# Two more buffers of sums in dead rows, an earlier load of 7x7 weights, and second statistics tile by tile, at the end of v

## The chip, the cores and the metric

One core of a Trainium2 chip runs the whole kernel. The metric is the device time of one execution in microseconds (us); four executions of the kernel before took 2723.07 to 2725.19 us, with a median of 2723.79 us. The engines are PE (matmul), PEld (its weight loads), DVE (vector), ACT (scalar), POOL (GpSimd) and SP; SP, ACT and POOL also issue DMA transfers, each in its own queue and in program order.

## The reference

The input x has 384 channels of 192x192 pixels, all in 32-bit floats. Two layers are added to it one after the other, each behind a group norm with 32 groups of 12 channels:

```python
x = x + attention_layer(group_norm(x))     # q, k, v at half size, top-k attention, GELU, projection
x = x + conv7(group_norm(x))               # depthwise 7x7, weights averaged over four rotations
```

The second norm needs mean and variance of the finished sum of the first layer, so the 7x7 convolution can't be corrected for it before the last sum is made. The kernel convolves the raw sums and folds the norm in: the weights get a multiple of the identity (the residual, scaled by the standard deviation), the results are multiplied by the reciprocal deviation, and the mean enters by the borders and by a row of offsets.

## The kernel before

Channels are cut into three tiles of 128 (KT = 3, index ot or kt). In the stage called v (from about 1390 to 2130 us of the span) the image is worked on in 16 groups of rows. For a group, `convolve` makes v by matmuls, `depthwise_v` (L1375, L1379) does nine taps on DVE, `attend` (L1441, L1448) multiplies by the attention matrix and applies GELU, `project` (L1465, L1473) makes y, and `residual` adds x: four DVE adds (L1502) write a block of sums into one of three buffers `sxs`, two ACT squares (L1522) read it for the variance, and two POOL transfers (L1543) store it to the DRAM tensor `sd`. A buffer is used again when its squares and its store are done. A row group and a tile make one block; they use the buffers in turn.

The last three row groups, numbers 14, 15 and 16 (the last is the first one of the circle again), form the drain: nine blocks, (14,0) to (16,2), with the squares of one group issued between the projections of the next. The rows that the taps read lie in `vrows`: three groups in the tile `rowbuf` (pool `rowp`), two in `rows2`. The pool context `bctx` is closed after the drain.

The last stage convolves 8 channels per step, 48 steps. A step loads `w` (the 7x7 weights as banded matrices, from `wt`), `h` (weights for halo rows, from `wh`), `main` (sums, from `sd`) and `aux` (halo rows, from `sh`), three buffers each; steps 0 and 1 load by SP, the others by ACT (`queue`, L1654). Before its matmuls, `middle` (L1752, DVE) adds the scaled identity to w, `borders` (L1817, L1829, L1837, L1844, POOL) fixes main and aux with the mean, `rest` (L1856, ACT) copies rows into aux and `columns` (L1676, L1677, ACT) copies weights from w to h. The matmuls (L1909) come in four groups q = 0 to 3 of two channels, three each: two with main, one with aux and h. DVE evacuates q = 0 and 2 (L1929), ACT q = 1 and 3 (L1927). `spread` (L1868, POOL) turns the result, and SP stores it. At q = 1 ACT and DVE do `middle`, `rest` and `columns` of the next step. At the head of step n stand the loads of step n + 2 and `borders` of step n + 1.

Between the two stages lie the statistics: sums over the squares and means per channel (L1714 to L1721), sums over the groups by matmuls with `gsel` (`over_groups`, L193: seven matmuls, each of two rows in the profile as all matmuls in 32 bits), `norm_of` (L219 to L223, a power on POOL at L222), then `along` (L1762, L1769, L1770), which spreads mean, deviation and reciprocal along the free dimension as mb, sb, rb, and `masked` (L1774), which makes mm. The offsets `offs` of all 384 channels are stored in one row of `wh` (L1807); for steps 0 and 1 they go straight into h (L1803). Matmuls with no use (`busy`, L1730) fill PE's pauses. `keep` holds an instruction in program order on its engine; other instructions are ordered by a scheduler, which lets filler matmuls and memsets slide forward.

Of the kernel before, what the change touches and what calls it, by code (L numbers as in the profile page):

```python
# [8 lines left out]
F32 = mybir.dt.float32  # L9
# [4 lines left out]
P = 128  # L14
# [45 lines left out]
TR = 32  # L60
# [26 lines left out]
def conv_preact_d2(  # L87
# [152 lines left out]
    bctx = ExitStack()  # L240
    rowp = bctx.enter_context(tc.tile_pool(name="rowp", bufs=1))
    ROW = (NT + 2) * (PS + 2)
# [1181 lines left out]
    for i in range(3):  # L1424
        t = sxp.tile([P, LEAD + CP * RB * RUN + LEAD], F32, name=f"sx{i}")
        nc.gpsimd.memset(t, 0.0)
        sxs.append(t)

    junk = wq[:, 0:2, 0 : RB * NT * NJ].rearrange("p k (n j) -> p k n j", j=NJ)

# [57 lines left out]
    def residual(i, ot, y, xr, pin):  # L1488

        b = order[i % NBC]  # L1490
        flat = sxs[(i * KT + ot) % len(sxs)]
        xq = xr.rearrange("p t (a j e) -> p a t j e", a=RB, e=CP)
# [102 lines left out]
    for j, dys in ((NBC - 2, (2,)), (NBC - 1, (0, 1))):  # L1595
        for ct in range(KT):
            depthwise_v(j, ct, dys[1:] if (j, ct) == (NBC - 1, 0) else dys, keep)
    before = [()] * KT
    for j in range(NBC - 2, NBC + 1):
# [12 lines left out]
        before = after  # L1612
# [13 lines left out]
    with ExitStack() as ex_:  # L1626

        fixed = ex_.enter_context(tc.tile_pool(name="fixed", bufs=1))
        wbufs = [fixed.tile([P, CB, 2 * P], F32, name=f"w_{i}") for i in range(3)]
        early = ex_.enter_context(tc.tile_pool(name="early", bufs=1))  # L1630
# [20 lines left out]
        def queue(n):  # L1651

            engine = nc.sync if n < 2 else nc.scalar
            return lambda dst, src: keep(engine.dma_start(dst, src))  # L1654

        for h in hbufs:
            nc.gpsimd.memset(h[0:TR, :, 2 * TR :], 0.0)
            nc.gpsimd.memset(h[REST:P, :, TR:], 0.0)  # L1660

        def load_w(n):
            w = wbufs[n % len(wbufs)]
            queue(n)(w, wt[:, span(n)])
            return w
# [60 lines left out]

        def busy(ps, n):

            for _ in range(n):
                keep(nc.tensor.matmul(ps[:, 0:H], wp[:, 0, 0:P], wp[:, 1, 0:H], start=True, stop=True))  # L1730
# [51 lines left out]

        idle = pc.tile([P, 2, 512], F32, name="idle", tag="pc")
        busy(idle[:, 0], 2)
        along(mb, mean1, 0)()
        busy(idle[:, 0], 2)
        masked(0)
        nc.vector.reciprocal(std1, rstd1)
        along(sb, std1, 0)()
        busy(idle[:, 0], 3)  # L1790
        middle(0)
# [4 lines left out]
        nc.vector.tensor_tensor(sumw, sumw, mean1, ALU.mult)  # L1796
        nc.vector.tensor_tensor(off1, mean0, std1, ALU.mult)
        nc.vector.tensor_tensor(off1, off1, sumw, ALU.subtract)

        offs = wide.tile([P, KT, P], F32, name="offs")  # L1800
        nc.vector.tensor_scalar_mul(offs[:, 0, :], ones, off1[:, 0:1])
        for n in ws:
            nc.sync.dma_start(ws[n][1][ONE : ONE + 1], offs[span(n), 0, :])  # L1803
        along(rb, rstd1, 0)()
        for kt in range(1, KT):
            nc.vector.tensor_scalar_mul(offs[:, kt, :], ones, off1[:, kt : kt + 1])
        nc.sync.dma_start(wh[ONE - TOP].rearrange("(t p) n -> p t n", p=P), offs)  # L1807

# [71 lines left out]
        borders(0)  # L1880
        rest(0)
        last = None

        later = {2 * kt: kt for kt in range(1, KT)}
        for n in range(steps):
            if n + 2 < steps:
                ws[n + 2] = load_w(n + 2), load_h(n + 2)
                mains[n + 2] = load_main(n + 2), load_aux(n + 2)
            if n + 1 < steps:
                borders(n + 1)  # L1890
            if last is not None:
                spread(n - 1, last)
            (w, h), (main, aux) = ws.pop(n), mains.pop(n)
# [111 lines left out]
```

## Time and profile before

| | |
|---|---|
| median of 4 executions | 2723.79 us |
| the profiled execution, its span | 2723.07 us, 2721.4 us |
| busy: PE, DVE, ACT, POOL | 92%, 83%, 52%, 54% |
| first adds of the drain (14,0); last adds (16,2) end | 2075.9; 2130.2 us |
| last square ends | 2131.6 us |
| first matmul of the last stage | 2143.5 us |
| last matmul of the last stage | 2710.4 us |
| mean granted clock of PE | 0.981 |

Times in the views are from the start of the span. A line of the timeline gives start, length, engine, line of the kernel, operation, tile written and tiles read, shapes and count; in brackets stands how long the engine was idle before it, and which instruction ended that. Engines with a q (SPq, ACTq) are issues of transfers. The windows give busy times in a stretch with PE's granted clock and the share and rate of the DMA engines. A matmul of 288 columns in 32 bits is two rows of 0.243 us at full clock.

### The profile page before, as it was taken

Reading aid. Unit: us, or ns where it says so; the run is one execution under the profiler, and the core shown is the slowest. Engines: PE = TensorE matmul, PEld = TensorE weight load, DVE = VectorE, ACT = ScalarE, POOL = GpSimd, SP = SyncE. Lnnn points to the kernel's source line nnn. Section 1 sums busy time; section 2 is a strip of 40 time slices with the busy share of each in tenths; the row PEclk is TensorE's granted clock in tenths of the full one; section 3 lists DMA queues with packets and bytes.
Section 4 is the critical chain, followed back from the end, with each engine's and each line's share of the span. In section 5 each row is a group of like instructions: output and inputs, shape, how many; then the busy total and the mean of one; then the engine's idle time right before and its main releaser. Section 6 shows DMA issues by size and latency. Waiting matters only on the chain. (4 is left out here: it accounts for less than half of the span.)

```text
span 2721.4 us, 29562 instructions
## 1 busy us (share of the span) xinstructions
PE 2510.6 (92%) x8893; PEld 1629.0 (60%) x8893; DVE 2247.4 (83%) x3161; ACT 1420.5 (52%) x2710; POOL 1467.7 (54%) x1588
## 2 busy tenths in 40 slices
PE   0299999999999999999889969999999799999998
PEld 0144566656666666655556636666666577777776
DVE  7985788888888888888689959898888779888876
ACT  0032667676767676776112213223224677777776
POOL 1013788888887988866122310101001578777787
PEclk9999999999999999999999979999999899999999
DMA  9962355454554554433429995766746999999998
GB/s 379 399 235 52 126 153 145 127 152 150 146 152 118 157 151 145 137 89 79 149 93 327 351 305 187 246 203 221 249 147 233 328 351 365 372 370 357 369 374 268
DMA packets 467582, 609.59 MB, mean 224 GB/s; under 512 B 250160, under 2 KB 399264, under 8 KB 450656
## 3 DMA queue, kind: packets, MB, share of 16 engines
q1 hardware_dynamic: 406928, 311.80, 36.9%
q0 software_dynamic: 37376, 148.85, 15.8%
q10 hardware_dynamic: 23120, 147.07, 14.5%
q8 instruction: 71, 1.16, 0.2%
q14 instruction: 87, 0.71, 0.1%
HBM read 370.93 MB, written 208.21 MB: 213 GB/s over the span
## 5 line engine op out<-in xcount | busy, mean ns | idle before, releaser
L563 PE MATMUL pv<-xv,wq 128*128 128x384 f32 x1512 | 500.8, 492 | 39.2 <-DMA xv<-in_x_dram 25.9
L1909 PE MATMUL pc<-main,w 128*128 128x288 f32 x1536 | 435.0, 405 | 3.6 <-issue 1.2
L563 PEld LDWEIGHTS pv<-xv,wq 128*128 128x128 f32 x1512 | 289.5, 192 | 242.4 <-issue 27.0
L1929 DVE TENSOR_SCALAR apart<-pc,rb 32x576 f32<-32x576 f32 x384 | 312.3, 813 | 98.4 <-PE pc L1909 84.8
L869 POOL TENSOR_TENSOR qk<-qk,more 128x384 f32<-128x384 f32 x290 | 309.8, 1074 | 109.7 <-ACT more L868 100.8
L1543 POOL DMA_DIRECT2D sd<-sx x96 | 72.4, 758 | 519.8 <-DVE sx L1502 498.3
L1927 ACT ACTIVATE apart<-pc,rb 32x576 f32<-32x576 f32 x384 | 281.4, 733 | 133.5 <-PE pc L1909 128.7
L1909 PEld LDWEIGHTS pc<-main,w 128*128 128x128 f32 x1536 | 289.7, 189 | 87.3 <-PE pc L1909 2.2
L1375 DVE SCALAR_TENSOR_TENSOR vb<-rows,wd,vb 128x576 f32<-128x576 f32 x384 | 312.8, 817 | 10.8
L869 POOL TENSOR_TENSOR qk<-qk,rows 128x384 f32<-128x384 f32 x216 | 230.5, 1072 | 76.2 <-ACT rows L868 70.0
L1909 PE MATMUL pc<-aux,h 128*128 128x288 f32 x768 | 248.8, 406 | 1.3 <-POOL aux L1844 1.3
L901 DVE SCALAR_TENSOR_TENSOR bank_r<-ring,wd,bank_r 128x384 f32<-128x384 f32 x383 | 236.2, 617 | 6.9
L1868 POOL COPY res<-apart 128x1152 f32<-128x1152 f32 (+1 forms) x96 | 216.5, 2283 | 37.8 <-DMA out_dram<-res 27.0
L1502 DVE TENSOR_TENSOR sx<-xr,y 128x576 f32<-128x576 f32 x180 | 203.7, 1172 | 25.2 <-ACT y L1473 15.0
L1009 PE MATMUL bank_b<-rows,more 128*128 128x384 f32 x528 | 220.4, 499 | 2.0 <-ACT bank_c L1111 1.1
L569 DVE TENSOR_REDUCE rows<-pv 128x192 f32<-128x768 f32 x144 | 137.7, 956 | 77.0 <-PE pv L563 76.9
L1522 ACT ACTIVATE wq<-sx,negmid 128x1152 f32<-128x1152 f32 x96 | 120.6, 1256 | 127.0 <-DVE sx L1502 122.7
L1089 DVE TENSOR_TENSOR rows<-bank_c,rows 128x384 f32<-128x384 f32 x132 | 73.2, 555 | 126.5 <-PE bank_c L1009 68.5
L1909 PEld LDWEIGHTS pc<-aux,h 128*128 128x128 f32 x768 | 144.6, 189 | 44.4 <-POOL aux L1844 2.6
L868 ACT ACTIVATE more<-ring,wd 128x384 f32<-128x384 f32 x290 | 170.3, 609 | 0.0
L1009 PE MATMUL bank_x<-xq,wq 128*128 128x384 f32 x378 | 154.7, 491 | 1.0 <-ACT bank_b L1061 1.0
L1009 PE MATMUL bank_y<-xq,wq 128*128 128x384 f32 x378 | 154.6, 491 | 0.0
(342 smaller groups left out, 4813.9 us busy)
## 6 DMA issues: line engine op xcount, KB each, us to landing
sd<-sx POOLq DMA_DIRECT2D x96, 600.0 KB, 10.3
out_dram<-res SPq DMA_DIRECT2D x192, 288.0 KB, 10.4
main<-sd ACTq DMA_DIRECT2D x46, 1200.0 KB, 7.8
xr<-in_x_dram SPq DMA_DIRECT2D x45, 1152.0 KB, 13.4
xq<-in_x_dram SPq DMA_DIRECT2D x21, 2304.0 KB, 8.5
xv<-in_x_dram SPq DMA_DIRECT2D x126, 384.0 KB, 7.9
w<-wt ACTq DMA_DIRECT2D x46, 1024.0 KB, 6.9
xs<-in_x_dram SPq DMA_DIRECT2D x24, 1536.0 KB, 15.2
```

What stands on the lines that cost most here:

```text
L563: nc.tensor.matmul(ps[:, u, 0 : RB * HW], wq[:, kt, o : o + P], xb[:, u, kt, :], start=(kt == 0), stop=(kt == KT - 1),)
L569: nc.vector.tensor_reduce(rows[ct][:, 1 + t0 : 1 + t0 + UT, 1 : PS + 1], ps[:, :, 0 : RB * HW].rearrange("p u (a w b) -> p u w a b", a=2, ...
L868: keep(nc.scalar.mul(part.rearrange("p (h w) -> p h w", w=PS), src, w))
L869: keep(nc.gpsimd.tensor_tensor(flat, flat, part, ALU.add))
L901: nc.vector.scalar_tensor_tensor(into, src, w, before, ALU.mult, ALU.add)
L1009: nc.tensor.matmul(ps[:, 0:HN], lhs, rhs, start=start, stop=True, skip_group_check=True)
L1375: pin(nc.vector.scalar_tensor_tensor(dst, src, w, dst, ALU.mult, ALU.add))
L1502: nc.vector.tensor_tensor(bass.AP(flat.tensor, flat.offset + at(e) + a * RUN, [flat.ap[0], [JP, NT], [1, NJ], [at(f) - at(e), 2]],), xq[:, ...
L1868: keep(copy(res[ps, k], apart[ps, :, k].rearrange("p e n -> p n e")))
L1909: nc.tensor.matmul(ahead[q][:, k, 0 : NT * NJ], lhs, rhs, start=(j == 0), stop=(j == 2), skip_group_check=True,)
L1927: keep(nc.scalar.mul(dst, src, scale))
L1929: keep(nc.vector.tensor_scalar_mul(dst, src, scale))
```

## The change

`rowp` moves from `bctx` to the context of the whole kernel, so that `rowbuf` stays. When its rows are dead, two buffers of sums are made in it (floats 0 to 2504 and 2504 to 5008) and the three `w` buffers (at 5008, 2504 and 0, 2048 floats each). The drain takes five buffers in turn instead of three. The load of w for step 0 is issued in the drain, ahead of the loads of x for group 16. The second statistics are split: group sums of tile 0 (two matmuls) and all that hangs on them come first; group sums of tiles 1 and 2 (five matmuls), their norm, the offsets and the store of the offsets to `wh` come in step 0, behind the first 8 matmuls. The loads of step n + 2 and `borders` of step n + 1 move behind them in the program. The h buffers are cleared one by one: the first ahead of `borders(0)`, the others behind it. The 16 filler matmuls before the sums go; six new ones read the sums of (16,1), and four stand between the spreads, which are reordered.

```diff
-    rowp = bctx.enter_context(tc.tile_pool(name="rowp", bufs=1))
+    rowp = ctx.enter_context(tc.tile_pool(name="rowp", bufs=1))
...
+    DRAIN = NBC - 2
+    SXN = LEAD + CP * RB * RUN + LEAD
+    WN = CB * 2 * P
+    places_w = (2 * SXN, SXN, 0)
...
-        flat = sxs[(i * KT + ot) % len(sxs)]
+        k = (i - DRAIN) * KT + ot
+        flat = sxs[k % len(sxs)] if k >= 0 else sxs[(i * KT + ot) % 3]
...
+    wbufs = [
+        rowbuf[:, o : o + WN].rearrange("p (c n) -> p c n", n=2 * P) for o in places_w
+    ]
+    sxs += [rowbuf[:, k * SXN : (k + 1) * SXN] for k in range(2)]
...
             y = project(j, ot, gl, keep)
+            if (j, ot) == (NBC - 1, 0):
+                keep(nc.sync.dma_start(wbufs[0], wt[:, 0:CB]))
+                for t in sxs[3:]:
+                    nc.gpsimd.memset(t, 0.0)
...
-        for h in hbufs:
-            nc.gpsimd.memset(h[0:TR, :, 2 * TR :], 0.0)
-            nc.gpsimd.memset(h[REST:P, :, TR:], 0.0)
+        def clear(h):
+
+            keep(nc.gpsimd.memset(h[0:TR, :, 2 * TR :], 0.0))
+            keep(nc.gpsimd.memset(h[REST:P, :, TR:], 0.0))
...
-            busy(gps.tile([P, 512], F32, name="busy"), 16)
-            ps = over_groups(gps, about(mv1, gmid, "1"), 2, "gs1")
-            norm_of(ps, gmid, mean1, rstd1, "1")
+        around = about(mv1, gmid, "1")
...
+        busy(idle[:, 0], 6, sxs[((2 * KT + 1) % len(sxs))][:, LEAD : LEAD + H])
+        group_sums(idle[:, 1], (0,))
+        normed1(idle[:, 1], 0, 1)
+        clear(hbufs[0])
+        busy(idle[:, 0], 1)
+        copied = [along(mb, mean1, 0)]
+        keep(nc.vector.reciprocal(std1[:, 0:1], rstd1[:, 0:1]))
+        busy(idle[:, 0], 1)
+        copied += [along(sb, std1, 0), along(rb, rstd1, 0)]
+        busy(idle[:, 0], 2)
+        copied[0]()
+        masked(0)
+        copied[1]()
+        middle(0)
+        copied[2]()
+        offset(0, 1)
...
         columns(0)
         borders(0)
         rest(0)
+        for h in hbufs[1:]:
+            clear(h)
...
         for n in range(steps):
-            if n + 2 < steps:
-                ws[n + 2] = load_w(n + 2), load_h(n + 2)
-                mains[n + 2] = load_main(n + 2), load_aux(n + 2)
-            if n + 1 < steps:
-                borders(n + 1)
-            if last is not None:
-                spread(n - 1, last)
...
             if n == 0:
                 for q in range(2):
                     sums(q, range(2))
+                group_sums(idle[:, 1], (1, 2))
+                normed1(idle[:, 1], 1, KT)
+                keep(nc.vector.reciprocal(std1[:, 1:], rstd1[:, 1:]))
+                offset(1, KT)
+                nc.sync.dma_start(wh[ONE - TOP].rearrange("(t p) n -> p t n", p=P), offs)
+            if n + 2 < steps:
+                ws[n + 2] = load_w(n + 2), load_h(n + 2)
+                mains[n + 2] = load_main(n + 2), load_aux(n + 2)
+            if n + 1 < steps:
+                borders(n + 1)
+            if last is not None:
+                spread(n - 1, last)
```

`group_sums` issues the matmuls of `over_groups` for the tiles named, `normed1` the five instructions of `norm_of` for these columns, and `offset` the three small DVE operations on off1 and one 128x128 DVE multiplication per tile into `offs`.

More of the change, by code (lines that the diff above doesn't have):

```diff
@@ L1597, in conv_preact_d2 @@
             depthwise_v(j, ct, dys[1:] if (j, ct) == (NBC - 1, 0) else dys, keep)
+    wbufs = [
+        rowbuf[:, o : o + WN].rearrange("p (c n) -> p c n", n=2 * P) for o in places_w
+    ]
+    sxs += [rowbuf[:, k * SXN : (k + 1) * SXN] for k in range(2)]
     before = [()] * KT
-    for j in range(NBC - 2, NBC + 1):
+    for j in range(DRAIN, NBC + 1):
         gl = attend(j, keep)
@@ L1626, in conv_preact_d2 @@
     with ExitStack() as ex_:
-        fixed = ex_.enter_context(tc.tile_pool(name="fixed", bufs=1))
-        wbufs = [fixed.tile([P, CB, 2 * P], F32, name=f"w_{i}") for i in range(3)]
         early = ex_.enter_context(tc.tile_pool(name="early", bufs=1))
@@ L1654, in queue @@
             return lambda dst, src: keep(engine.dma_start(dst, src))
-        for h in hbufs:
-            nc.gpsimd.memset(h[0:TR, :, 2 * TR :], 0.0)
-            nc.gpsimd.memset(h[REST:P, :, TR:], 0.0)
+        def clear(h):
+            keep(nc.gpsimd.memset(h[0:TR, :, 2 * TR :], 0.0))
+            keep(nc.gpsimd.memset(h[REST:P, :, TR:], 0.0))
         def load_w(n):
             w = wbufs[n % len(wbufs)]
-            queue(n)(w, wt[:, span(n)])
+            if n > 0:
+                queue(n)(w, wt[:, span(n)])
             return w
@@ L1725, in conv_preact_d2, with busy @@
         rstd1 = const.tile([P, KT], F32, name="rstd1")
-        def busy(ps, n):
+        def busy(ps, n, rhs=wp[:, 1, 0:H]):
             for _ in range(n):
-                keep(nc.tensor.matmul(ps[:, 0:H], wp[:, 0, 0:P], wp[:, 1, 0:H], start=True, stop=True))
+                keep(nc.tensor.matmul(ps[:, 0:H], wp[:, 0, 0:P], rhs, start=True, stop=True))
         with tc.tile_pool(name="gps1", bufs=1, space=PSUM) as gps:
@@ L1783, in conv_preact_d2 @@
         idle = pc.tile([P, 2, 512], F32, name="idle", tag="pc")
[L1784 to L1791, printed above, removed]
+        g1 = const.tile([P, KT, 2], F32, name="norm_1")
         sumw = const.tile([P, KT], F32, name="sumw")
@@ L1795, in conv_preact_d2, with group_sums @@
         off1 = const.tile([P, KT], F32, name="off1")
-        nc.vector.tensor_tensor(sumw, sumw, mean1, ALU.mult)
-        nc.vector.tensor_tensor(off1, mean0, std1, ALU.mult)
-        nc.vector.tensor_tensor(off1, off1, sumw, ALU.subtract)
         offs = wide.tile([P, KT, P], F32, name="offs")
-        nc.vector.tensor_scalar_mul(offs[:, 0, :], ones, off1[:, 0:1])
+        def group_sums(ps, jts):
+            for jt in jts:
+                kts = [kt for kt in range(KT) if abs(jt - kt) < 2]
+                for kt in kts:
+                    keep(
+                        nc.tensor.matmul(
+                            ps[:, 2 * jt : 2 * jt + 2],
+                            gsel[:, kt, jt * P : (jt + 1) * P],
+                            around[:, kt, :],
+                            start=(kt == kts[0]), stop=(kt == kts[-1]),
+                        )
+                    )
@@ new lines, in normed1 @@
+        def normed1(ps, lo, hi):
+            g = g1[:, lo:hi]
+            r = rstd1[:, lo:hi]
+            src = ps[:, 2 * lo : 2 * hi].rearrange("p (t n) -> p t n", n=2)
+            keep(nc.vector.tensor_scalar_mul(g, src, 1.0 / GC))
+            keep(nc.vector.tensor_tensor(r, g[:, :, 0], g[:, :, 0], ALU.mult))
+            keep(
+                nc.vector.scalar_tensor_tensor(
+                    r, g[:, :, 1], GN_EPS, r, ALU.add, ALU.subtract
+                )
+            )
+            keep(nc.gpsimd.tensor_tensor(r, r, halfneg[:, lo:hi], ALU.pow))
+            keep(nc.vector.tensor_tensor(mean1[:, lo:hi], gmid[:, lo:hi], g[:, :, 0], ALU.add))
@@ new lines, in offset @@
+        def offset(lo, hi):
+            o, w = off1[:, lo:hi], sumw[:, lo:hi]
+            keep(nc.vector.tensor_tensor(w, w, mean1[:, lo:hi], ALU.mult))
+            keep(nc.vector.tensor_tensor(o, mean0[:, lo:hi], std1[:, lo:hi], ALU.mult))
+            keep(nc.vector.tensor_tensor(o, o, w, ALU.subtract))
+            for kt in range(lo, hi):
+                keep(nc.vector.tensor_scalar_mul(offs[:, kt, :], ones, off1[:, kt : kt + 1]))
+        busy(idle[:, 0], 6, sxs[((2 * KT + 1) % len(sxs))][:, LEAD : LEAD + H])
@@ L1802, in conv_preact_d2 @@
+        group_sums(idle[:, 1], (0,))
[13 more added lines that the diff above has]
+        offset(0, 1)
         for n in ws:
             nc.sync.dma_start(ws[n][1][ONE : ONE + 1], offs[span(n), 0, :])
-        along(rb, rstd1, 0)()
@@ L1805, in conv_preact_d2 @@
-        for kt in range(1, KT):
-            nc.vector.tensor_scalar_mul(offs[:, kt, :], ones, off1[:, kt : kt + 1])
-        nc.sync.dma_start(wh[ONE - TOP].rearrange("(t p) n -> p t n", p=P), offs)
         def borders(n):
```

## The prediction

> **What bounds the kernel now.** The busy table says 92% PE, which tells nothing of the place that is changed, so I read the slices first, then the timeline of 2050 to 2170 us engine by engine, then the windows around it, and last the transfers with their landings. Before 2096 and after 2143.5 PE has no gap worth a microsecond. Between them a chain over DVE, ACT and POOL sets the pace, and it has two parts. First the drain, on DVE:
>
> ```profile
> 2096.52 8.96 DVE L1502 TENSOR_TENSOR sx<-xv,y 128x576 f32<-128x576 f32 x8
> 2111.26 4.63 DVE L1502 TENSOR_TENSOR sx<-xv,y 128x576 f32<-128x576 f32 x4 [5.77 <-ACT wq L1522]
> 2116.79 9.99 DVE L1502 TENSOR_TENSOR sx<-xr,y 128x576 f32<-128x576 f32 x9 [0.91 <-DMA sd<-sx]
> ```
>
> Four adds of 1.1 us make one block of sums. After eight, DVE stands for 5.77 us. The view names ACT, but the squares of that buffer were long done; the second half of its store to sd was issued at 2097.73 and landed 13.4 us later, at 2111.13. So it is the third buffer that is missing. Then the second part, from the last square to the first matmuls:
>
> ```profile
> 2130.27 1.26 ACT L1522 ACTIVATE wq<-sx,negmid 128x1152 f32<-128x1152 f32 x1 [0.86 <-DVE about L211]
> ...
> 2132.42 3.15 PE L193 MATMUL gs<-about,gsel 128*128 128x2 f32 x14 [16.66 <-DVE about L213]
> ...
> 2136.59 0.88 POOL L222 TENSOR_TENSOR rstd<-rstd,halfneg 128x3 f32<-128x3 f32 x1
> ...
> 2139.10 0.82 DVE L1774 TENSOR_TENSOR mm<-mb,mask 128x640 f32<-128x640 f32 x1
> ...
> 2140.71 2.10 POOL L1829 COPY aux<-main 32x2304 f32<-32x2304 f32 x1
> ...
> 2141.16 3.04 DVE L1752 SCALAR_TENSOR_TENSOR w<-eye,sb,w 128x512 f32<-128x512 f32 x2
> ...
> 2143.47 4.12 PE L1909 MATMUL pc<-main,w 128*128 128x288 f32 x16 [0.99 <-POOL aux L1829]
> ```
>
> Every row here waits for the one above it. Squares end at 2131.62, mm ends at 2139.92 (8.30 later), the aux matmuls start at 2147.52 (7.60 later; they wait for ACT's L1856, which ends at 2147.42). The third place is what ACT does next:
>
> ```profile
> 2144.33 0.34 ACTq L1654 DMA_DIRECT2D w<-wt  x1
> 2144.88 0.40 ACT L1677 COPY h<-w 32x256 f32<-32x256 f32 x1
> 2145.30 2.12 ACT L1856 COPY aux<-main 32x2304 f32<-32x2304 f32 x1
> 2146.74 0.52 ACTq L1654 DMA_DIRECT2D h<-wh  x1
> 2147.74 0.34 ACTq L1654 DMA_DIRECT2D main<-sd  x1
> 2148.12 0.52 ACTq L1654 DMA_DIRECT2D aux<-sh  x1
> 2149.79 2.97 ACT L1927 ACTIVATE apart<-pc,rb 32x576 f32<-32x576 f32 x4 [2.37 <-PE pc L1909]
> 2152.77 2.12 ACT L1856 COPY aux<-main 32x2304 f32<-32x2304 f32 x1
> 2154.90 0.62 ACT L1676 COPY h<-w 32x512 f32<-32x512 f32 x1
> ```
>
> The load of h for step 2 stands until 2146.74. The store wh<-offs was issued by SP at 2140.22 and takes 6.5 us to land: 2146.72. So this load, in ACT's queue, waits for that store, and ACT's evacuation L1927 and the copies of step 1 (L1856, L1676, L1677) stand behind it. Now that costs nothing, as the matmuls of q=1 end later anyway. Step 1's aux matmuls start at 2156.33, 8.81 after those of step 0, just after its copies.
>
> **Part by part.** I sum from aux matmuls to aux matmuls, since from step 1 on PE is gapless (11.64 us a step to the end, some 6 us of gaps in all), so what is gained or lost there reaches the end whole.
>
> A. Two more buffers. DVE has no wait: the blocks that would reuse a buffer need stores of 2080.8, 2085.3 and 2097.0 (landed by 2091.7, 2096.7 and 2111.1) at 2105.5, 2110 and 2114.4. DVE ends its adds at 2105.5 + 4 x 4.46 = 2123.4 instead of 2130.18. ACT is then the later one: from 2106.23 on it needs per block two squares (2.63) and a pair of y (0.95), so 3 x 3.58, 2 x 2.63, 1.37, and a last 1.37 that must wait for DVE: 2125.0 instead of 2131.62. **-6.6**. The two memsets (6.75 us for three at L1426, so 2.25 each) stand in POOL's order ahead of the stores of iterations 11 and 15 of the loop over row groups; POOL waits some 36 us per iteration for DVE's adds there, and DVE's L1375 took its usual 0.81 beside the earlier memsets: nothing. If POOL were busy, the store behind would be 2.25 later. The load of w0 moves on SP ahead of the last xr loads; its buffer is free when DVE's row taps end (about 2073.5), the DMA share is 0.00 from 2066 to 2080, and xr can't go before 2080.5: nothing, and 1 MB leaves the crowded stretch 2102 to 2122 (share 1.02).
>
> B. Statistics of one tile. Of 14 PE rows (3.15 us at a granted clock of 0.50) 4 stay: 0.5 (0.117 a row as in gs_mid at full clock) to 0.9 (0.213): -2.4. The power no longer stands behind six memsets: 2136.16 to 2136.59, -0.4. mb's matmul is behind one filler instead of two (its diagonal was ready at 2136.6, PE came to it at 2137.97): -0.6. **-3.4**; mm then ends at 2125.0 + 4.9 = 2129.9. main0 must be there: its load waits for the store of block (16, 0). Behind the 8.3 MB ahead of it at 366 GB/s that lands near 2122.7 (2128.0 before), main0 near 2130: 0 to +1.
>
> C. From mm to the aux matmuls. The w update L1752 needs 0.74 at its fastest row and 2.2 beside POOL's copy L1829; now it starts before that copy, so the first matmuls come 1.3 to 3.5 after mm (3.55 before). But then PE does 10 rows of the other tiles' sums (1.2), and rest(0) still ends some 7.3 after mm. 7.3 to 8.7, I take 8.0, the middle: **+0.4**. Aux matmuls at 2137.9, 9.6 earlier.
>
> D. The other tiles' statistics behind the first matmuls, and the store with them. wh<-offs now needs the second sums (done about when aux starts), POOL's power behind borders(0) and four memsets (2.5 us, POOL free at some 2138.3), 0.9 for it and 1.2 for DVE's offsets: SP issues the store 2.9 after the aux start, where it was 7.3 before it. Landing: 1.6 to 1.9 us for the small transfers at 1383 us with idle engines, 6.5 for this very store behind main1. By my count main1 has landed by 2139 and the store comes at 2140.8, so 2.2, near the low row; both ends are kept. Then ACT: 2.1 to issue h, main and aux (2146.74 to 2148.84), evacuation 2.97, L1856 2.12, L1676 and L1677 1.03, 0.1: step 1's aux matmuls 2.9 + 2.2 + 8.3 = 13.4 after step 0's, where 8.81 was enough. **+4.6** (+4.0 to +8.9). This is the price of the change: a wait that was covered becomes the one that ends last.
>
> [...]
>
> E. PE's clock. PE then stands 4.6 us in step 1. In this trace the granted clock fell 2.0 us after PE's last matmul (2094.06 to 2096.1) and 4.3 after (2115.75 to 2120), and came back 4.3 after work resumed (2098.66 to 2103) or 8.1 after (2132.42 to 2140.5):
>
> ```profile
> 2098.60:2103.00 4.40, 4.34 (x9) 3.20 (x10) 4.33 (x5) 1.29 (x6) 1.50 (x2) 0.50 0.89 293
> 2103.00:2120.00 17.00, 12.75 (x52) 9.42 (x50) 10.19 (x10) 13.05 (x29) 3.00 (x4) 1.00 1.03 368
> 2120.00:2140.50 20.50, 7.74 (x25) 6.54 (x26) 15.00 (x45) 7.34 (x12) 10.23 (x19) 0.50 0.90 322
> ```
>
> (stretch, length, busy times with counts of PE, PEld, DVE, ACT and POOL, clock, DMA share, GB/s.) Half speed for 4.3 us loses 2.2, for 8.1 4.0, no fall loses 0. I take **+2.0**, near the first row.
>
> [...]
>
> Sum: -6.6 - 3.4 + 0.4 + 4.6 + 2.0 = **-3.0**. The profiled execution took 2723.07 (span 2721.4 and 1.67 outside), 0.72 below the median 2723.79; -3.0 makes 2720.1 of it and **2720.8** as a median. Lowest ends: -6.6 - 3.6 - 0.3 + 4.0 + 0 = -6.5; highest: -6.6 - 2.2 (group sums at 0.9, main0 a us late) + 1.1 + 8.9 + 4.0 = +5.2. What a measurement of this kernel can tell from no change is taken as 0.2%, 5.4 us.
>
> **Rivals.**
> R1, the gain arrives whole: the load of h doesn't hold ACT, or is not late. For it: SP is free, the DMA engines are idling by then. Against: 2146.72 and 2146.74 above, and the order in which the changed kernel issues on ACT: the four loads stand ahead of the evacuation. Then D and E are nearly 0: -9.6 + about 1 = 2715.
> R2, slower: the store lands late, since it stands on SP behind w1, aux1 and main1 while w2 comes in on ACT. Price: each us of landing over 2.2 is a us of PE. The loss begins at 5.2, passes 0.2% at about 10.6; w at 2097.60 took 13.2: +11.0, 2731.8. Against: it carries 192 KB and comes after the crowd.
> R3, the buffers do not remove the wait, because sd stores only queue on full DMA engines (share 1.02) and main0 is as late as before, 2135.5 by the bytes: aux at 2143, 4.6 earlier instead of 9.6: -4.6 + 4.6 + 2.0 = +2.0, 2725.8.
>
> **How the numbers follow.** Forecast (a gain and its return, -6.5 to +5.2) 0.74; R1 0.12, R2 0.06, R3 0.08. The predicted time is 2720.8. The range 2716 to 2728.5 covers the forecast and R3 and leaves out R1 and R2. Faster by over 0.2%: R1 and 0.05 from the forecast's low end, 0.17. Slower: R2 and 0.02 from its high end, 0.08. Within: 0.75.
>
> **What would show it.** A: no DVE gap over 0.3 in the drain, squares ending near 2125. B and C: 4 sum rows, mm near 2130, aux near 2138. D: a h load on ACT at the landing of wh<-offs, L1927 of q=1 right behind it, and a PE pause of 4 to 5 us in step 1, released by ACT's h copy (L1691). E: a clock near 0.5 after it. If PE has no pause there, or one above 8, the forecast is wrong; so it is if main0 lands after 2133.

## The result, and the profile after

The changed kernel took 2729.69 us (median of 38 executions) against 2723.61 us of the kernel before in the same sessions (59 executions): ratio 1.0021, 95% interval 1.0017 to 1.0026. It is slower by 5.7 us; the forecast was 2720.8 us, and the time lies above its range of 2716 to 2728.5 us. The profiled execution has a span of 2726.6 us and a mean clock of 0.979.

The drain starts 2.0 us earlier in this execution (first adds of (14,0) at 2073.90, before 2075.93), so I measure everything below from these first adds. Such a time is written d+...: the last square ends at d+50.0 (before d+55.7), mm at d+55.2 (d+64.0), step 0's aux matmuls start at d+70.7 (d+71.6), those of step 1 at d+84.7 (d+80.4), step 10 at d+195.1 (d+188.7). PE is 9 us ahead when mm is made, 1 us ahead at the aux matmuls, and 4 us behind one step later.

The timeline of DVE answers the first three lines of before. The adds that stood 5.77 us for a buffer now follow directly; the gap left is a wait for ACT's y.

```profile
2099.71 3.38 DVE L1508 TENSOR_TENSOR rows<-xv,y 128x576 f32<-128x576 f32 x3
2102.94 4.64 DVE L1508 TENSOR_TENSOR sx<-xv,y 128x576 f32<-128x576 f32 x4
2108.62 9.11 DVE L1508 TENSOR_TENSOR sx<-xr,y 128x576 f32<-128x576 f32 x8 [1.05 <-ACT y L1478]
```

The timelines of SP, POOL and PE show the second part, from the squares to the first matmuls (SPq lines, and the first one of POOL, are issues of transfers; the first line issues the last two stores, those of (16,2)):

```profile
2122.31 1.50 POOL L1549 DMA_DIRECT2D sd<-rows  x2 [2.77 <-DVE mask L1713]
...
2124.64 1.02 PE L1809 MATMUL idle<-about,gsel 128*128 128x2 f32 x4 [3.95 <-DVE about L213]
2125.03 0.34 SPq L1666 DMA_DIRECT2D main<-sd  x1
...
2126.33 0.57 POOL L1829 TENSOR_TENSOR rstd<-rstd,halfneg 128x1 f32<-128x1 f32 x1 [1.87 <-DVE mean L1830]
...
2131.71 1.49 SPq L1858 DMA_DIRECT2D h<-offs  x2
...
2136.30 0.65 POOL L1868 TENSOR_TENSOR main<-main,mm 128x48 f32<-128x48 f32 x2 [8.13 <-DMA main<-sd]
...
2136.65 5.74 PE L1955 MATMUL pc<-main,rows 128*128 128x288 f32 x16 [6.05 <-POOL main L1868]
2142.23 1.17 PE L1809 MATMUL idle<-about,gsel 128*128 128x2 f32 x10
2144.55 2.18 PE L1955 MATMUL pc<-aux,h 128*128 128x288 f32 x8 [1.15 <-DMA h<-offs]
```

Four rows of sums and a power of 0.57 us are there as forecast, and mm ends at 2129.12. But POOL then stands 8.13 us for main of step 0, a wait that the kernel before did not have: there the same instruction came straight behind mm.

```profile
2140.00 0.65 POOL L1817 TENSOR_TENSOR main<-main,mm 128x48 f32<-128x48 f32 x2 [2.53 <-DVE mm L1774]
```

PE's first 16 rows take 5.74 us instead of 4.12, since its clock has fallen (0.50 from 2136 to 2139), and then the aux matmuls wait 1.15 us for 4 KB of offsets that SP issued at 2131.71, behind w, aux and main of step 1.

The third part, in the timelines of SP, ACT and PE, is as forecast:

```profile
2148.16 0.37 SPq L1969 DMA_DIRECT2D wh<-offs  x1
2150.34 0.53 ACTq L1666 DMA_DIRECT2D h<-wh  x1
...
2152.38 2.97 ACT L1985 ACTIVATE apart<-pc,rb 32x576 f32<-32x576 f32 x4 [13.29 <-DVE rows L1764]
2155.36 2.12 ACT L1907 COPY aux<-main 32x2304 f32<-32x2304 f32 x1
2157.49 0.62 ACT L1690 COPY h<-rows 32x512 f32<-32x512 f32 x1
2158.62 1.30 PE L1955 MATMUL pc<-aux,h 128*128 128x288 f32 x2 [5.07 <-issue]
```

The store of the offsets lands at 2150.32, ACT's load of h leaves at 2150.34, and the evacuation and the copies stand behind it. The view names a DVE write for ACT's 13.29 us, but that was done long before; what ended the wait was the load ahead of it in ACT's own order. PE stands 5.07 us, and its first rows afterwards take 0.48 us each.

The windows show the clock (the last column but two, after the busy times of PE, PEld, DVE, ACT and POOL; then DMA share and GB/s) in three stretches where PE comes back from a pause:

```profile
2125.00:2130.00 5.00, 4.75 (x17) 3.88 (x17) 3.78 (x12) 0.00 (x0) 1.78 (x3) 0.53 1.05 259
...
2136.00:2145.00 9.00, 7.20 (x28) 5.70 (x29) 0.67 (x6) 2.12 (x1) 7.83 (x12) 0.78 0.88 368
...
2157.00:2163.80 6.80, 5.18 (x11) 3.78 (x12) 0.95 (x2) 4.42 (x7) 6.26 (x8) 0.50 0.71 255
```

In the first, which opens within the sums, the clock is near half behind 3.95 us without work; in the second main's 16 rows start at half clock, behind 6.05 us (0.52 from 2138 to 2140, 1.00 from 2140 to 2141); the third lies behind the pause of 5.07 us in step 1, and PE works 5.18 us of it at half clock.

### The profile page after: what moved, and what is told of

Same layout as the page of the kernel before. It is cut to its first block, busy times and chain, and to the rows that moved or that the text cites. A ratio compares the mean times of both kernels' runs of the same rounds, so it can differ in the third digit from the quotient of the medians.

```text
span 2726.6 us, 29520 instructions
## 1 busy us (share of the span) xinstructions
PE 2512.4 (92%) x8867; PEld 1628.5 (60%) x8867; DVE 2223.3 (82%) x3169; ACT 1420.2 (52%) x2710; POOL 1475.0 (54%) x1591
## 5 line engine op out<-in xcount | busy, mean ns | idle before, releaser
L1955 PE MATMUL pc<-main,rows 128*128 128x288 f32 x1536 | 437.9, 408 | 8.4 <-POOL main L1868 6.0
L1955 PEld LDWEIGHTS pc<-main,rows 128*128 128x128 f32 x1536 | 292.1, 190 | 92.7 <-POOL main L1868 6.5
L869 POOL TENSOR_TENSOR qk<-qk,rows 128x384 f32<-128x384 f32 x216 | 230.6, 1072 | 76.1 <-ACT rows L868 69.9
L1528 ACT ACTIVATE wq<-sx,negmid 128x1152 f32<-128x1152 f32 x90 | 113.1, 1256 | 119.5 <-DVE sx L1508 116.0
L1955 PEld LDWEIGHTS pc<-aux,h 128*128 128x128 f32 x768 | 145.0, 190 | 50.4 <-issue 6.1
```

The source lines that it names most:

```text
L869: keep(nc.gpsimd.tensor_tensor(flat, flat, part, ALU.add))
L1955: nc.tensor.matmul(ahead[q][:, k, 0 : NT * NJ], lhs, rhs, start=(j == 0), stop=(j == 2), skip_group_check=True,)
```

## The experiments

**How to read them.** The median of the kernel before differs from chip to chip (2709 to 2723 us in these sessions), so each ratio is to the kernel before on the same chip, with its 95% interval; its half width is about 0.0013, or 3.5 us. The changed kernel was not run again beside the experiments; where one is compared with its 1.0021, this ratio is taken to hold on every chip. The traces resolve more up to step 10: PE milestones there differ by whole microseconds. This table gives them, after the drain's first adds, from each kernel's timeline:

| kernel | squares end | mm ends | POOL takes main 0 | aux 0 | aux 1 | step 10 | ratio |
|---|---|---|---|---|---|---|---|
| before | 55.7 | 64.0 | 64.1 | 71.6 | 80.4 | 188.7 | 1 |
| changed | 50.0 | 55.2 | 62.4 | 70.7 | 84.7 | 195.1 | 1.0021 |
| e1 h(2) by SP | 49.6 | 54.5 | 61.1 | 70.6 | 80.4 | 188.9 | 1.0008 |
| e3 undivided | 48.6 | 56.3 | 60.2 | 69.9 | 80.4 | 188.1 | 0.9995 |
| e4 three buffers | 52.4 | 57.7 | 57.8 | 68.9 | 79.7 | 188.1 | 1.0007 |
| e5 fillers | 49.6 | 54.4 | 60.1 | 69.8 | 82.9 | 191.3 | 1.0020 |
| e6 main 0 ahead | 49.8 | 54.7 | 55.7 | 66.2 | 82.8 | 192.0 | 1.0029 |
| e7 e6 and e1 | 50.0 | 55.2 | 55.6 | 66.3 | 77.8 | 185.9 | 0.9996 |
| e9 loads first | 50.1 | 55.3 | 55.5 | 66.2 | 77.8 | 189.2 | 1.0001 |
| e10 three, offs on ACT | 53.0 | 58.3 | 58.4 | 67.5 | 78.4 | 187.0 | 1.0006 |
| e11 five, offs on ACT | 49.7 | 54.5 | 61.0 | 68.4 | 80.4 | 190.4 | 1.0012 |
| e12 w early | 52.6 | 57.9 | 58.7 | 66.4 | 78.1 | 186.1 | 0.9992 |
| e13 e12, main 2 early | 52.5 | 57.7 | 57.9 | 68.4 | 79.8 | 188.7 | 0.9988 |
| e14 e12, undivided | 52.7 | 60.4 | 60.5 | 69.1 | 79.4 | 188.0 | 0.9988 |

### The wait on ACT, the split and the clock

**e1.**

```diff
 def load_h(n):
...
-    queue(n)(h[TOP:REST], wh[:, span(n)])
+    queue(min(n, 1) if n == 2 else n)(h[TOP:REST], wh[:, span(n)])
```

> The changed kernel, with one load moved: h of step 2 is issued by SP, behind the store of the offsets, and no longer by ACT. Theory (the wait on ACT is the price): in the changed kernel ACT stood until that store had landed (2150.32) and its evacuation of q=1 and the copies of step 1 came after it. Without it step 1's aux matmuls come 8.8 us after those of step 0, as in the kernel before, not 14.07, and PE doesn't stand 5.0 us, so its clock doesn't fall either (2.9 us more): 8.2 us less, 2721.5 against 2729.7, ratio to the kernel before 0.9992. Rival (step 1 is late by itself, since main and aux of step 1 land late and POOL ends its borders at 2150.05): the pause shrinks by 2 us at most and the time is about 2727.7.

Measured: 1.0008 (0.9995 to 1.0020). Up to step 0's aux matmuls it is the changed kernel (d+70.6); step 1's follow after 9.8 us, and step 10 starts 6.2 us earlier than in the changed kernel. The timelines of ACT and PE:

```profile
2136.34 2.98 ACT L1985 ACTIVATE apart<-pc,rb 32x576 f32<-32x576 f32 x4 [8.93 <-PE pc L1955]
...
2143.92 0.72 PE L1955 MATMUL pc<-aux,h 128*128 128x288 f32 x2 [0.57 <-POOL aux L1888]
```

ACT now waits for PE, not for a landing, and PE's pause of 5.07 is 0.57. The wait on ACT is shown. Against the changed kernel's 1.0021 the median gains 0.13%, 3.5 us and not 8.2, with an interval that does not reach 8.2.

**e3**, the statistics undivided as in the kernel before, with the five buffers and all else changed:

```diff
-        group_sums(idle[:, 1], (0,))
-        normed1(idle[:, 1], 0, 1)
+        group_sums(idle[:, 1], range(KT))
+        normed1(idle[:, 1], 0, KT)
...
+        nc.sync.dma_start(wh[ONE - TOP].rearrange("(t p) n -> p t n", p=P), offs)
...
```

> The changed kernel with the second statistics undivided: the seven sums of all tiles, the norm, all offsets and their store ahead of step 0. Theory: the store lands before ACT comes to the load of h for step 2, nothing is held, PE has no pause in step 1 and the DMA engines aren't left at a share of 0.31 between 70 and 80 us: 4 to 6 us less than the changed kernel, ratio to the kernel before 0.9998 to 1.0008, and the aux matmuls of step 0 are no later than the 70.65 us of the changed kernel, since main of step 0 set them. Rival (the split gains what mm gains, 3 us): 1.002 to 1.003.

Measured: 0.9995 (0.9985 to 1.0006), 0.26% better than the changed kernel. The aux matmuls of step 0 are not later than with the split (d+69.9 against d+70.7), as main of step 0 sets them, and step 1's come at d+80.4. The load of h for step 2 still waits for the store (2131.41, a landing of 9.8 us, against 2.15 in the changed kernel), but by then ACT has nothing to do; the timeline of ACT:

```profile
2131.41 0.52 ACTq L1666 DMA_DIRECT2D h<-wh  x1
...
2134.98 2.97 ACT L1981 ACTIVATE apart<-pc,rb 32x576 f32<-32x576 f32 x4 [10.83 <-PE pc L1956]
```

So the split, with the store that it moves, is the part that made the change slower. It brings mm 2.5 us sooner after the squares (5.2 us against 7.7; in this execution the squares themselves end 1.4 us earlier), which bought nothing, as main was late, and it made the wait on ACT the last one.

**e5**, fillers in PE's pause:

```diff
+            if n == 1:
+                ahead[0] = pc.tile([P, 2, 512], F32, name="pc1_0", tag="pc")
+                busy(ahead[0][:, 0], 9)
...
```

> The changed kernel with nine matmuls of no use (two rows each, some 4.4 us at full clock) ahead of step 1's matmuls, inside PE's pause of 5.07 us. Theory (the clock falls in that pause and costs 2.4 to 2.9 us after it): from step 1's first aux matmul to the first matmul of step 3 the changed kernel took 26.84 us, the kernel before 24.38; with the fillers it takes 24.4 to 24.6, step 1's aux start stays at 84.7 us after the drain's first adds, and the end comes 2.4 earlier, ratio to the kernel before 1.0012 instead of 1.0021. [...]

Measured: from step 1's first aux matmul to step 3 24.1 us (26.8 in the changed kernel): PE's rows stay at full speed (granted clock 1.00 from 2149 to 2160), as its timeline shows.

```profile
2144.78 4.53 PE L1744 MATMUL pc<-wp 128*128 128x288 f32 x18
2149.14 1.13 PE L1958 MATMUL pc<-main,rows 128*128 128x288 f32 x4
2150.13 0.72 PE L1958 MATMUL pc<-aux,h 128*128 128x288 f32 x2
```

The clock's price, 2.7 us here, is shown on PE. The ratio is 1.0020 (1.0004 to 1.0036), so that it reaches the end is not shown.

### Main of step 0

**e4**, the three old buffers, all else as changed:

```diff
-        flat = sxs[k % len(sxs)] if k >= 0 else sxs[(i * KT + ot) % 3]
+        flat = sxs[(i * KT + ot) % 3]
...
-    sxs += [rowbuf[:, k * SXN : (k + 1) * SXN] for k in range(2)]
...
```

> The changed kernel with the three old buffers of sums only, all else as changed. Theory (main of step 0 sets the first matmuls, and it waits for bytes in the DMA queues, not for the adds): the squares end about 6 us later, 55.7 us after the drain's first adds, mm about 61, main lands some 60 to 62 after them, so the first aux matmuls are no later than the 70.6 of the changed kernel: time 2728 to 2730.5, no worse than 2729.7 by more than 1. Rival (the earlier squares are worth what they save): everything behind them is 5.7 us later, 2735.4.

Measured: 1.0007 (0.9993 to 1.0022). The squares end 2.4 us later and mm 2.5 later, yet main of step 0 is there when POOL wants it (d+57.8 against d+62.4), and the aux matmuls start 1.8 us earlier than with five buffers. Timeline of PE:

```profile
2118.26 1.83 PE L1740 MATMUL idle<-wp 128*128 128x288 f32 x4
2119.93 4.04 PE L1951 MATMUL pc<-main,rows 128*128 128x288 f32 x16
2123.81 1.17 PE L1805 MATMUL idle<-about,gsel 128*128 128x2 f32 x10
2129.28 4.17 PE L1951 MATMUL pc<-aux,h 128*128 128x288 f32 x8 [4.30 <-DMA h<-offs]
```

The load of main is issued at d+50.4 here and at d+51.1 in the changed kernel: nearly the same. What differs is what stands before it. With three buffers the stores of (16,2) are issued at d+51.3, behind it; with five all stores of (16,1) and (16,2) are issued by d+49.2, ahead of it. The timelines of SP and POOL in e4:

```profile
2110.80 0.34 SPq L1662 DMA_DIRECT2D main<-sd  x1
...
2111.70 1.50 POOL L1548 DMA_DIRECT2D sd<-sx  x2 [3.76 <-DVE mask L1709]
```

e4 shows a second thing. Its squares end at d+52.4, 3.3 us before those of the kernel before, which has three buffers too. The wait for the third buffer is there, but it is 1.88 us and not 5.77, as the timeline of DVE shows:

```profile
2091.90 4.68 DVE L1507 TENSOR_TENSOR sx<-xv,y 128x576 f32<-128x576 f32 x4 [1.88 <-DMA sd<-sx]
```

The store that it waits for was issued at d+21.8 in both kernels and landed after 9.6 us here, after 13.4 in the kernel before. Of the edits left in e4 only one touches transfers up to there: w of step 0, 1 MB, is loaded at d-2.4 and not at d+21.7, just ahead of that store.

**e6** puts main of step 0 ahead of these stores, which `late` holds; **e7** is e6 with the edit of e1.

```diff
+    main0 = rows2[:, 0:MN].rearrange("p (c t j) -> p c t j", c=CB, j=JP)
+    keep(nc.scalar.dma_start(main0.rearrange("p c t j -> p c (t j)"), sd[:, 0:CB]))
+    for dst, src in late:
+        keep(nc.scalar.dma_start(dst, src))
...
```

> The changed kernel, with main of step 0 loaded by ACT's queue right behind the squares, and the sums of (16,1) and (16,2) stored by ACT's queue behind that load, no longer by POOL ahead of it; w, aux and main of step 1 follow on ACT's queue. Main of step 0 and the first two h lie in the dead rows of the second row tile so that the load can stand there. The load of h for step 2 still stands on ACT. Theory (main of step 0 was held by the stores in POOL's queue): it is issued near 2125 as before but has the DMA engines for itself: 1.18 MB at 368 KB a us is 3.2 us, with 2.2 us as the offsets' store took it lands at 2130.4, not 2136.1; POOL's borders and the first matmuls come 5.7 earlier, the offsets in h don't stand behind main of step 1 any more, and the aux matmuls start near 2138, 6.5 earlier; the wait in step 1 stays: 2723.2. Rival (the load is slow by itself, 11 us whoever is ahead): it lands near 2136 again and the time is 2729.7.

> Both edits together: main of step 0 ahead of the last stores, and h of step 2 loaded by SP behind the store of the offsets. Theory (the two losses are separate and add): 2729.7 - 8.2 - 6.5 = 2715.0, below the kernel before by 8.6 us, ratio 0.9968. Rival (they overlap, since one chain sets the start of step 1 in both): the better of the two alone, 2721.5.

Measured: in e7 the load is issued at d+48.9 and lands at d+55.4, after 6.5 us instead of 11, in e6 after 6.75; the aux matmuls of step 0 start at d+66.2 and d+66.3, 4.4 us earlier than in the changed kernel. The transfers in the window from issue to landing, first of the changed kernel (2125 to 2130, its first five microseconds), then of e7 (2117.3 to 2123.8); columns are packets, MB and the share of the 16 engines:

```profile
DMA packets 299, 1.30 MB, mean 259 GB/s; under 512 B 32, under 2 KB 32, under 8 KB 296
...
q0 software_dynamic: 296, 1.27, 103.3%
q1 hardware_dynamic: 3, 0.03, 2.1%
```

```profile
DMA  0000099650119899799695999849929276999999
...
q10 hardware_dynamic: 452, 1.60, 80.9%
```

q0 is POOL's queue, q1 SP's, q10 ACT's. For five microseconds after main was issued on SP, POOL's stores took 1.27 of 1.30 MB; in the next two (2130 to 2132) SP's queue moved 0.41 MB and POOL's 0.18. In e7, where nothing stood ahead, the first bytes moved five slices of 0.16 us after the issue. So in these five microseconds SP's queue, which carries main, moved 0.03 MB, and sharing began only behind them; why POOL's queue came first for so long, no run here shows. e6 and e7 also move main and the stores to ACT's queue; e4 changes the order and not the queues.

The ratio of e6 is 1.0029 (1.0016 to 1.0042), not the gain expected: the wait on ACT is still in it (aux 1 at d+82.8). e7 is 0.9996 (0.9983 to 1.0009), 0.25% better than the changed kernel, 6.8 us where 14.7 were expected. In both, aux of step 0 came late: SP issued it only near d+55.5 (probably since its new place in memory was not free before), and POOL waited 5 us for it.

**e10 and e11** put the offsets into h by ACT's queue, with three and five buffers (both with the edit of e1):

```diff
-            nc.sync.dma_start(ws[n][1][ONE : ONE + 1], offs[span(n), 0, :])
...
+            keep(nc.scalar.dma_start(ws[n][1][ONE : ONE + 1], offs[span(n), 0, :]))
```

> The run with three buffers of sums, with the offsets of steps 0 and 1 put into h by ACT's queue and not by SP's behind main of step 1, and h of step 2 loaded by SP. Times after the drain's first adds. Theory: with three buffers the stores of (16,2) come 0.9 us after the issue of main of step 0 and not ahead of it, so main is there when mm ends (57.7); the only wait left ahead of the aux matmuls was for those 4 KB (68.86), so these start at 64.8; step 1's follow at 73.9, set by main of step 1 (68.9) and POOL's 5 us of borders; step 10 at 182.5, 6.2 less than in the kernel before, ratio 0.9977. Rival (h waits for all that is in flight, whichever queue carries it): aux matmuls at 68.9 again, step 10 at 186 to 188.

> The same two queue moves on the changed kernel with its five buffers. Times after the drain's first adds. Theory (the two more buffers put four stores of the last blocks ahead of main of step 0): main lands at 61 to 62.4 again, PE, gone to half clock, takes 6.0 us for the 16 rows and 1.2 for the sums, aux matmuls at 68.7, step 1's at 77.5, step 10 at 185.9; so five buffers are some 3.4 us worse than three, ratio 0.9990. Rival (earlier squares win once the other waits are gone): five buffers are better than three by 2.5 to 3.2 us, the difference of the squares.

Measured: aux 0 at d+67.5 and d+68.4, aux 1 at d+78.4 and d+80.4; ratios 1.0006 (0.9992 to 1.0021) and 1.0012 (0.9999 to 1.0024). Three buffers are better on PE by 0.9, 2.0 and, at step 10, 3.4 us, as the first theory says; the medians do not resolve it. The move of the 4 KB gained 1.4 of the 4.1 us expected.

**e9** loads main of steps 0 and 1 and w of step 1 ahead of all late stores.

```diff
+    for n, m in enumerate(early_mains):
+        keep(nc.sync.dma_start(m.rearrange("p c t j -> p c (t j)"), sd[:, n * CB : (n + 1) * CB]))
+        if n == 0:
+            keep(nc.sync.dma_start(wbufs[1], wt[:, CB : 2 * CB]))
+    for dst, src in late[1]:
+        keep(nc.sync.dma_start(dst, src))
...
```

> Main of steps 0 and 1 (in the dead second row tile) and w of step 1 are loaded by SP ahead of the stores of (16,1), and these ahead of aux of step 1 and the stores of (16,2); h of steps 0 and 1 and aux of step 0 go by POOL's queue, the offsets into h by ACT's, h of step 2 by SP's. Times after the drain's first adds. Theory (order in the DMA queues decides, the bytes are the same): main of step 0 is issued at 49.0 and lands at 55.5, as in the run with main ahead of the stores; mm ends at 55.2; aux matmuls start 7 after mm, as with three buffers they could have, 62.2; main of step 1 lands near 60.5, so step 1's aux matmuls come 8.8 later, 71.0; step 10 starts at 179.3 against 188.7 in the kernel before: 9.4 us less, ratio 0.9965. Rival (the delayed stores come back as a later wait): w of step 2 waits for the store of (16,2), and PE stands in step 2 for up to 4 us, step 10 at 183, ratio 0.998.

Measured: 1.0001 (0.9989 to 1.0014). Main of step 0 lands after 5.3 us at d+51.3, yet the aux matmuls start at d+66.2 only: the offsets were issued at d+59.8 and landed 6 us later. Step 1 is 2.6 us ahead of the kernel before, step 10 0.5 us behind it. So 3.1 us are lost between step 1 and step 10 (111.4 us against 108.3). That is the rival: w of step 2, behind the store of (16,2), left at 2132.34 and its main at 2132.96.

### What sets the steps that follow

Gains at step 1 seemed not to reach the end, so I asked what sets steps 3 to 47.

**f1** leaves out a twelfth of PE's rows.

```diff
                     for j in steps:
+                        if j == 2 and q == 3 and n >= 3:
+                            continue
...
```

> The changed kernel without the third matmul (aux with h) of the last two channels in steps 3 to 47: four of a step's 48 PE rows less, 0.97 us a step, 43.7 us in all, with the same transfers. Theory (from step 1 on the DMA engines set the time: their share is 0.99 to 1.03 from 100 us after the drain's first adds to the end in every run so far, and a step's 4.3 MB at 370 KB a us take 11.6 us, as long as its 48 rows): the time stays within 5 us of the changed kernel's, ratio to the kernel before 1.000 to 1.003. Rival (PE sets the last stage, as the prediction had it): 40 to 44 us less, ratio 0.986.

Measured: 1.0027 (1.0014 to 1.0041). PE does 43.7 us less work, and nothing is gained: PE alone is not the bound there. The windows show its idle time beside a full DMA share:

```profile
2400.00:2450.00 50.00, 46.27 (x187) 34.95 (x188) 37.47 (x41) 38.44 (x48) 39.73 (x37) 1.00 1.01 361
2450.00:2500.00 50.00, 45.46 (x185) 34.27 (x183) 35.09 (x43) 35.99 (x44) 41.59 (x38) 1.00 1.01 365
```

**f2 and f3** leave out the loads of aux from step 3 on, in the changed kernel and in the one before (`if n < 3:` ahead of the load).

> The changed kernel without the loads of aux from step 3 on (0.6 MB of a step's 4.3 MB; the old halo rows stay in the buffers). Theory (the DMA engines set the time): with 3.7 MB a step they need 10.0 us where PE needs 11.64; the gaps of PE in steps 3 to 47 (some 4 to 8 us beyond 45 x 11.64 = 523.8) and the late last stores go, and the time is 6 to 10 us less than the changed kernel's: ratio to the kernel before 0.9985 to 1.0000. Rival (PE sets the time): less than 3 us less.

> The kernel before without the loads of aux from step 3 on. Theory (the DMA engines set the time of the last stage, and only without that what step 0 and 1 gain or lose on PE reaches the end whole): 6 to 10 us less than the kernel before, ratio 0.9965 to 0.998; and the changed kernel with the same edit is slower than this one by what PE's rows are late at step 3, 4.9 to 6.8 us. Rival (PE sets the time in both): 0 to 3 us less than the kernel before.

Measured: 1.0069 (1.0054 to 1.0084) and 1.0043 (1.0030 to 1.0055), slower by 0.4 to 0.5% than with the loads. ACT's issue of main took longer, 1.10 us on average between 2200 and 2650 in f2 and 0.95 in f3, against 0.75 and 0.66 with the loads of aux; but all of ACT's loads of a step together took less time to issue than with them (2.2 us against 2.9 for f2), so this does not explain it. With seven transfers a step instead of eight the loads may wait for other earlier transfers than before; that is not shown, and the cause stays open. These two tell nothing of bytes.

**f4 and f5** keep the transfer and cut its rows, in the changed kernel and in the one before; **f6** is f4 with the edit of f1.

```diff
+            k = TOP + 8 if n > 2 else REST
-            queue(n)(aux.rearrange("p c t j -> p c (t j)")[TOP:REST], sh[:, span(n)])
+            queue(n)(aux.rearrange("p c t j -> p c (t j)")[TOP:k], sh[0 : k - TOP, span(n)])
```

> The changed kernel with aux loaded for 8 of its 64 halo rows from step 3 on (75 KB instead of 600; the rest stays from before), so that each step still has eight transfers. Theory (DMA engines are the bound): 3.8 MB a step need 10.3 us where PE needs 11.64, so PE's gaps in steps 3 to 47 go and the late stores too: 5 to 10 us less than the changed kernel, ratio to the kernel before 0.9985 to 1.0003. Rival (bytes don't matter, or transfers with few rows are as slow): at or above 1.0021.

> The same edit on the kernel before. Theory: PE without gaps from step 3 on ends 4 to 8 us earlier, ratio 0.997 to 0.9985, and the changed kernel with this edit is slower than this one by PE's delay at step 3, 4.9 to 6.8 us. Rival: 1.000 or above.

> The changed kernel with both cuts: no third matmul of the last two channels from step 3 on (0.97 us of PE's 11.64 a step) and aux loaded for 8 of 64 halo rows (3.8 MB a step instead of 4.3, 10.3 us at 370 KB a us). Theory (PE and the DMA engines are two limits at the same pace): now both need some 10.3 to 10.7 us a step and 30 to 43 us go: ratio to the kernel before 0.987 to 0.991. Rival (a third limit sets the pace, as POOL's copies that wait for the stores of results, or ACT's and DVE's evacuation): 1.000 to 1.003 again.

Measured: 1.0023 (1.0014 to 1.0033), 1.0001 (0.9988 to 1.0013) and 0.9989 (0.9973 to 1.0005). An eighth of a step's bytes less changes nothing either, so the time does not follow the bytes, and my theory fell in the form in which I put it. But the edit did not free the DMA engines. The windows of the changed kernel, of f4 and of f6:

```profile
2200.00:2650.00 450.00, 448.09 (x1845) 347.38 (x1844) 352.80 (x391) 342.64 (x419) 357.44 (x337) 1.00 1.01 366
...
2200.00:2650.00 450.00, 448.19 (x1836) 345.87 (x1837) 396.00 (x385) 342.34 (x420) 360.22 (x343) 1.00 0.97 322
...
2200.00:2650.00 450.00, 423.13 (x1695) 315.68 (x1694) 399.88 (x386) 344.89 (x423) 363.05 (x343) 1.00 0.97 322
```

The rate falls by 12%, from 366 to 322 GB/s, but the engines' share only from 1.01 to 0.97. In f4 PE is as busy as in the changed kernel (448 of 450 us), so PE alone can set the pace there; in f1 it was the DMA engines that stayed full. Both cuts together gain 0.34% against f4, about 9 us of the 30 to 43 expected: PE then idles 27 of 450 us, beside a share of 0.97. So there are several limits at almost the same pace, and no run here took the DMA engines well below full. In the waits from 2200 to 2650, POOL stands for the stores of results in f1, and for main in f6:

```profile
POOL res L1919 <- DMA out_dram<-res: 51.5, 25, 5.3
```

```profile
POOL main L1869 <- DMA main<-sd: 70.1, 29, 5.1
```

(total us, times, longest.) Which one sets the pace once PE has less to do was not settled.

**e12, e13, e14** look for a version that beats both: e10 with w of steps 1 and 2 loaded at the drain's start; that with main and aux of step 2 on SP behind main of step 1 (the last line); e12 with undivided statistics.

```diff
+    for n in (2, 1):
+        keep(nc.sync.dma_start(wbufs[n], wt[:, n * CB : (n + 1) * CB]))
...
+        mains[2] = load_main(2), load_aux(2)
```

> The run with three buffers and the offsets on ACT's queue, with w of steps 1 and 2 loaded by SP at the drain's start into the dead rows, when the DMA engines have a share of 0.76. Theory (bytes moved in the first 100 us after the drain's first adds decide: 30.5 MB in the kernel before, 28.4 in the changed one, 31.4 in the run this is made from): up to 2 MB more are moved there, 32.5 to 33.4 MB, and the time is 5 to 8 us below the kernel before: ratio 0.997 to 0.998. Rival (w ahead of the loads of x delays the drain by what it saves later): ratio 1.000 to 1.001, with DVE waiting for x in the drain.

> The run with w of steps 1 and 2 loaded early, and with main and aux of step 2 loaded by SP right behind main of step 1, no longer by ACT behind its copies. Theory: in that run the DMA engines had a share of 0.35 between 70 and 80 us after the drain's first adds, 6.5 us idle; now these 1.8 MB fill it, PE's work is the same, and the end comes 4 to 6 us earlier: ratio to the kernel before 0.9970 to 0.9980 against 0.9992. Rival (idle DMA time there is of no account): 0.9992 again.

> Three buffers of sums, w of steps 0 to 2 loaded early, the offsets into h by ACT's queue, h of step 2 by SP's, and the second statistics undivided. Theory: mm ends 1 us later than with the split (58.9 us after the drain's first adds), the aux matmuls of step 0 start at 67, those of step 1 8.8 to 9.5 later, 76 to 76.5 instead of 78.1, as DVE and POOL have no sums, power and offsets to do ahead of step 1; step 10 at 184.5, ratio to the kernel before 0.998 to 0.999. Rival (the split's earlier start of step 0 is worth more): step 1 at 78 or later, ratio 0.9992 or above.

Measured: 0.9992 (0.9982 to 1.0002), 0.9988 (0.9975 to 1.0001), 0.9988 (0.9974 to 1.0002). All three beat the changed kernel by 0.3%; none is told from the kernel before. e13 did not help PE (aux 1 at d+79.8 against d+78.1), and in e14 mm came 2.5 us later, not 1, so its theory on PE fell too.

## Why the prediction was wrong, by its own steps

**A, two more buffers (-6.6): near in size, wrong in what it is put down to.** The squares end 5.7 us earlier in the drain's frame. But e4, without the two buffers, has 3.3 of them, and the edit left for it there is the earlier load of w, which the prediction put at nothing (no run moves that load alone). The buffers bring 2.4 us beside e4, and 2.3 to 4.4 between the other rows of the table. That both together come near the 6.6 is luck. The gap of 1.05 us behind ACT's y is over the 0.3 that A allowed. The memsets cost nothing: the first stores of the drain leave at d+4.9 in both kernels.

**B, statistics of one tile (-3.4): right for mm, wrong for main.** mm ends 5.23 us after the squares, 3.07 less than before. The step that failed is the last sentence: the store of block (16, 0) "lands near 2122.7 (2128.0 before), main0 near 2130: 0 to +1". With the 2.03 us between the two drains added, its two stores landed at 2125.5 and 2126.9, up to 4 us late, and main at 2138.2, 8 us late; that it lands after 2133 is the prediction's own sign of being wrong. I counted the bytes ahead of the store of (16,0) and gave the load behind it an idle DMA. The stores of (16,1) and (16,2), 2.4 MB, are ahead of that load too, and it is A that puts them there: buffers that no longer hold the adds no longer hold the stores. e4 (three buffers: main in time, although the adds are later) and e6 and e7 (stores behind the load: 6.5 to 6.75 us instead of 11) show it. This is the half of rival R3 that I gave 8 in 100; its price was counted with aux at 2143, and it was 2146.6 with the same 2.03 us.

**C, mm to aux (8.0): wrong, by the same cause.** It took 15.4: 7.2 until POOL had main, 7.1 for the 16 rows and the sums, these rows at a clock of 0.50 until 2139, and 1.15 for the offsets behind main of step 1. So 0.9 us of the 9.6 are left at the aux matmuls. One reading behind C was also wrong: not every row of the second view waits for the one above it. The update of w at 2141.16 waited for the copy of sb, which ended at 2141.13, and not for POOL's copy above it.

**D, the store and ACT (+4.6): right.** Issue 3.6 us after the aux start (2.9 forecast), landing 2.15 (2.2), aux to aux 14.07 (13.4): +5.3. e1, which takes the load off ACT, and e3, which stores ahead of step 0, show it. One premise held by luck: main of step 1, counted as landed by 2139, landed at 2147.0 with the 2.03 us added, 8 us late, but the store is issued behind the aux start, which was late as well.

**E, the clock (+2.0): right, a little small.** The third window shows 5.18 us of work at half clock, which lose 2.6 us; the prediction took 2.0, near half of 4.3. From aux 1 to step 3 the changed kernel lost 2.5 us against the one before, and e5's fillers bring back 2.7.

**The rivals.** R1 (the gain arrives whole) fell with the wait on ACT, and R2 (a late store) with the landing of 2.15 us.

**The sum.** With -0.9 for A to C, +5.3 and +2.5 PE is 6.8 us late at step 3 and 6.4 at step 10; the median says 5.7. Of the 9.8 us between the forecast of -3.0 and these 6.8, 7.4 lie between mm and the aux matmuls (15.4 instead of 8.0), where the wait for main that B put at 0 to +1 took 7.2; 1.2 are missing from A and B at mm (8.8 us earlier instead of 10.0), and D and E are 0.7 and 0.5. The sum's own highest end, +5.2, makes 2729.0, which the stated range up to 2728.5 left out already. The premise that "what is gained or lost there reaches the end whole" held for this loss within the interval. For gains it is not shown: e7 and e12 start step 10 2.7 to 2.8 us before the kernel before, and their medians are 0.04 and 0.08% below it, with intervals that reach no change; and f1 shows that PE's relief alone gains nothing. Had main been in time, the forecast's -3.0 might have shrunk for that reason; this stays open.

## What to carry to other kernels

A buffer that holds a producer also holds its stores: when you add buffers, list every transfer that now leaves earlier and what it overtakes, above all the load that the next stage starts with. Before moving a store behind some work, look up who loads its bytes, on which queue that load stands, and what is queued behind it. When two edits are meant to save the same wait, run each alone: here the earlier load seems to have done about as much as the two buffers. And measure what limits a stage by relieving one engine alone, and see in the profile that it is relieved, before you count microseconds won at its start.

## What the runs showed of the hardware that was not expected

- In the changed kernel POOL's queue, which had a backlog, kept the DMA engines nearly to itself for five microseconds after a load was issued on SP (1.27 of 1.30 MB from 2125 to 2130); then the two shared them (SP 0.41 and POOL 0.18 MB from 2130 to 2132).
- 4 KB of offsets, issued at 2131.71 behind main of step 1 on one queue, held PE's aux matmuls until 2144.55; the 192 KB store on the same queue, when it was empty, landed in 2.15 us.
- One load less per step made the kernel 0.4 to 0.5% slower (f2 and f3 against the changed kernel and the one before), and the cause stays open. An eighth less bytes with the same count of transfers made no difference (f4, f5), and the share of the DMA engines fell only from 1.01 to 0.97.
